# Turning layer 0's output by VectorE and DRAM instead of TensorE, in a block loop with given orders for three engines

## The chip, the cores and the metric

The kernel runs on one core of one Trainium2 chip. The metric is the device time of one execution in microseconds, as the median of several runs. TensorE (PE in the profile, its weight loads PEld), VectorE (DVE), ScalarE (ACT), GpSimd (POOL) and SyncE (SP) run their own instruction streams in order and wait for each other by semaphores. Transfers go through DMA queues; nearly all of this kernel's are issued by SyncE.

## The reference

Four layers over 128 graphs of 64 nodes with 256 features (8192 tokens), each with a residual and a layer norm. Only layers 0 and 1 are touched here:

```
# layer 0: dense graph attention
Wh = x @ W;  e = leaky(s1[:, None] + s2[None, :]);  e[adj == 0] = -inf
x = layernorm(x + softmax(e) @ Wh)
# layer 1: attention over 512 edges, 4 heads
q, v = x @ W_lin.T, x @ W_val.T
e = sum_d a * leaky(q[src] + q[dst])  + log(adj[src, dst] + 1e-8)
attn = softmax of e over the edges of one src
x = layernorm(x + segment_sum(attn * v[dst], src) @ W_out.T)
# layer 2: two batch-normed matmuls; layer 3: two graph convolutions and four small LSTMs
```

Layer 1's matmuls contract over features, so they need layer 0's output with features on the partitions, while layer 0 leaves it with tokens on the partitions. That turn is what the change is about.

## The kernel before

The 8192 tokens are cut into 16 blocks q of 512 tokens (8 graphs). Layers 0 and 1 and the start of layer 2 are one software pipeline over these blocks, from 0 to about 543 us; layer 2's matmuls and layer 3 follow and are the same in both kernels.

Layer 0 of a block is five steps. `l0_a` gives the input with features on partitions (`xT`): transfers have laid 32x32 squares of x in place in `A[:, q]`, and one VectorE instruction turns each square (L220). `l0_b` is x @ W (L230), `l0_c` the scores and their exponentials (L241 on TensorE, L244 to L248 on VectorE, L251 on ScalarE), `l0_d` transposes the exponentials on TensorE (L260) and copies them out (`eT`, L262), `l0_e` multiplies (L270), adds the residual (L273) and norms (L92 to L97). The norm's statistics are VectorE's, its power (L83) and its application (L97) GpSimd's. The result x1 stays in `A[:, q]`.

Layer 1 of a block: `l1_t` transposes x1 by eight PE transposes (L204) and two ScalarE copies (L205). `l1_qv` makes queries and values of half a block (L295, L298; copies L305 to L308). `l1_graph`, eight times a block, makes q[src] + q[dst] of one graph (`z`, L332) and its relu on ScalarE (`u`, L334). `sums` reduces four of them over the features (L323). Every second block, the softmax of the last two blocks follows: `l1_softmax` (L342 on TensorE, then a serial VectorE chain L344 to L351 with two scans, and the exponential L352), `l1_sums` (two more scans, L357 and L358) and `l1_weights` (transposes L366, reciprocal L372, product L374, four scattering transfers from GpSimd, L378, into a table in DRAM, and the load of the table back, `ld`, L384). Three to four blocks later come `v_a` (GpSimd copies the attention out of `ld` into `am`, L391; TensorE multiplies by the values, L399; ScalarE copies to `yT`, L403), `v_b` (L413, the residual add L415, the norm, the write of x2 to DRAM L418) and `v_c` (L433, copied into `A[:, q]` by L437).

The steps of a block are written out by hand: after each of the eight `l1_graph` calls b = 0 to 7 stands a short list of steps, called slot b here.

```
                [(l0_e, q + 1), (l0_a, q + 2)],
                [(sums, q if q else -1), (l1_softmax, S)],
                [(l1_sums, S), (l0_b, q + 2)],
                [(v_b, q - LAG - 1)],
                [(l1_weights, S), (l1_t, q + 1), (l0_c, q + 2)],
                [(sums, q), (l1_qv, q + 1, 0)],
                [(v_c, q - LAG - 1), (v_a, q - LAG)],
                [(l0_d, q + 2), (l1_qv, q + 1, 1)],
```

`step` holds each step behind the last TensorE instruction of the step before. The other engines' instructions are put in order by the scheduler that builds the program, by its own costs. It also picks the PSUM bank of each tile: the name "m" has three banks, "z" two, "e" one.

`A` is one tile of 16 x 1024 numbers per partition. `A[:, q]` serves in turn as the place for x's squares, for x1 and for layer 2's input. All plain transfers of the loop are issued by SyncE, in program order.

Of the kernel before, what the change touches and what calls it, by code (L numbers as in the profile page):

```python
# [17 lines left out]
P = 128  # L18
# [23 lines left out]
def kernel(ctx: ExitStack, tc: tile.TileContext, i, out):  # L42
# [69 lines left out]
    with ExitStack() as two:  # L112
# [13 lines left out]
        def load_x(q):  # L126
            xin[q] = xp.tile([P, PQ, D], F32, name="xin")
            nc.sync.dma_start(xin[q], x_view[q])
            if q:

                rows = i["x"][q * QT:(q + 1) * QT, :].rearrange("(j t) (k i f) -> i k t j f", t=32, k=KD, f=32)
                for n in range(4):
                    for k in range(KD):
                        to = A[n * 32:(n + 1) * 32, q, k * QT:(k + 1) * QT]
                        nc.sync.dma_start(to.rearrange("t (j f) -> t j f", f=32), rows[n, k])

        class su:

# [27 lines left out]
        for s in range(2):  # L166
            nc.sync.dma_start(bd[s * N:(s + 1) * N, s * N:(s + 1) * N], i["adj"])
        load_x(1)

        wq = wa.tile([P, KD, D + HEADS], F32, name="wq")  # L170
        wv = wa.tile([P, KD, D], F32, name="wv")
# [42 lines left out]

        def l0_a(q):
            L0[q] = {"x": xin.pop(q)}
            if q:

                L0[q]["xT"] = work.tile([P, KD, QT], F32, name="tT", bufs=1)
                nc.vector.transpose(L0[q]["xT"].rearrange("p k t -> p (k t)"), A[:, q, :])  # L220
            else:
                L0[q]["xT"] = transposed(L0[q]["x"], q)

        def l0_b(q):
            xT = L0[q]["xT"]
            wh = L0[q]["wh"] = own(q, [P, PQ, D + 2], "wh")
            for c in range(PQ):
                p_ = bank([D + 2])
                for k in range(KD):
                    nc.tensor.matmul(p_, xT[:, k, c * P:(c + 1) * P], w0[:, k, :],  # L230
                                     start=k == 0, stop=k == KD - 1)
                nc.scalar.activation(wh[:, c, :], p_, AF.Copy)

            sb = L0[q]["sb"] = own(q, [P, PQ, P], "sb")
            nc.scalar.activation(sb, wh[:, :, D + 1:].to_broadcast([P, PQ, P]), AF.Copy)

        def l0_c(q):
            wh, sb = L0[q]["wh"], L0[q]["sb"]
            sc = bank([PQ, P])
            for c in range(PQ):  # L240
                nc.tensor.transpose(sc[:, c, :], sb[:, c, :], ident)  # L241
            e = L0[q]["e"] = work.tile([P, PQ, P], F32, name="e0")
            for c in range(PQ):
                nc.vector.scalar_tensor_tensor(e[:, c, :], sc[:, c, :], wh[:, c, D:D + 1], mask,  # L244
                                               op0=OP.add, op1=OP.add)
            nc.vector.scalar_tensor_tensor(e, e, SLOPE, e, op0=OP.mult, op1=OP.max)
            mx = small.tile([P, PQ], F32, name="mx")
            nc.vector.tensor_reduce(mx, e, AX.X, OP.max, negate=True)  # L248
            sm = small.tile([P, PQ], F32, name="sm")
            for c in range(PQ):  # L250
                nc.scalar.activation(e[:, c, :], e[:, c, :], AF.Exp, bias=mx[:, c:c + 1],  # L251
                                     accum_out=sm[:, c:c + 1])
            ri = L0[q]["ri"] = small.tile([P, PQ], F32, name="ri")
            nc.vector.reciprocal(ri, sm)

        def l0_d(q):
            e = L0[q]["e"]
# [4 lines left out]
            nc.scalar.activation(eT, p_, AF.Copy)  # L262

        def l0_e(q):
            x, wh, eT, ri = (L0[q][n] for n in ("x", "wh", "eT", "ri"))
            for c2 in range(2):
                p_ = bank([2, D])
                for c in range(2):
                    g = 2 * c2 + c
                    nc.tensor.matmul(p_[:, c, :], eT[:, g, :], wh[:, g, :D], start=True, stop=True)  # L270
                for c in range(2):
                    g = 2 * c2 + c
                    nc.vector.scalar_tensor_tensor(x[:, g, :], p_[:, c, :], ri[:, g:g + 1], x[:, g, :],  # L273
                                                   op0=OP.mult, op1=OP.add)
            layernorm(token_major(q), x, PQ, nc.gpsimd)
            L0.pop(q)
            if q + 2 < NQ:
                load_x(q + 2)

# [1 line left out]
        L1 = {}  # L281

        def l1_t(q):
            L1[q] = {"xT": transposed(token_major(q)), "qs": [],
                     "v": vp.tile([P, PQ, D], F32, name="v", bufs=5)}

        def l1_qv(q, c2):
            xT, v = L1[q]["xT"], L1[q]["v"]
# [3 lines left out]
            for c in (2 * c2, 2 * c2 + 1):  # L292
                pq = bank([D + HEADS])
                for k in range(KD):
                    nc.tensor.matmul(pq, xT[:, k, c * P:(c + 1) * P], wq[:, k, :],  # L295
                                     start=k == 0, stop=k == KD - 1)
                for k in range(KD):
                    nc.tensor.matmul(pv[:, c % 2, :], xT[:, k, c * P:(c + 1) * P], wv[:, k, :],  # L298
                                     start=k == 0, stop=k == KD - 1)

                qs = work.tile([P, 2, D], F32R, name="qs", bufs=6)
# [37 lines left out]
        def l1_softmax(S):  # L339
# [9 lines left out]
            nc.vector.tensor_tensor_scan(up, seg[:, :E], e, NEG, OP.add, OP.max)  # L349
            nc.vector.tensor_tensor_scan(dn[:, ::-1], seg[:, 1:][:, ::-1], up[:, ::-1], NEG, OP.add, OP.max)  # L350
            nc.vector.tensor_sub(e, e, dn)  # L351
            nc.scalar.activation(e, e, AF.Exp)  # L352
            sm[S] = e, up, dn

        def l1_sums(S):
            e, up, dn = sm[S]
# [27 lines left out]
                nc.sync.dma_start(ld[S][s * N:(s + 1) * N], half)  # L384


        def v_a(q):
            S, b = divmod(q, BPS)
            v = L1[q]["v"]
            am = vp.tile([P, PQ * HEADS, N], F32, name="am")  # L390
            nc.gpsimd.tensor_copy(am.rearrange("p (e r) n -> p e r n", e=2),  # L391
                                  ld[S].rearrange("p n (e b r) -> p b e r n", e=2, b=BPS)[:, b])
            pY = [bank([KD, PQ, N]) for _ in range(2)]
            for c in range(PQ):
                for h in range(HEADS):
# [242 lines left out]
        LAG = BPS + 1  # L638


        queue = []

        def step(do, n, *more):
            if not 0 <= n < NQ:
                return
            traced = nc.cur_bb.bb.instructions
            first = len(traced)
            if queue:
                with tc.issue_after(queue[-1]):
                    do(n, *more)  # L650
            else:
                do(n, *more)
            mine = [t for t in traced[first:] if t.engine == mybir.EngineType.PE]
            queue.extend(mine[-1:])

        def sums(q):
            reduce_heads([pend.pop(0) for _ in range(min(4, len(pend)))])
# [1 line left out]
        for q in range(NQ):  # L659
            S = q // BPS - 1 if q % BPS == 0 else -1  # L660
            between = [
                [(l0_e, q + 1), (l0_a, q + 2)],
                [(sums, q if q else -1), (l1_softmax, S)],
                [(l1_sums, S), (l0_b, q + 2)],
                [(v_b, q - LAG - 1)],
                [(l1_weights, S), (l1_t, q + 1), (l0_c, q + 2)],
                [(sums, q), (l1_qv, q + 1, 0)],
                [(v_c, q - LAG - 1), (v_a, q - LAG)],
                [(l0_d, q + 2), (l1_qv, q + 1, 1)],
            ]  # L670
            for b in range(GQ):
                step(l1_graph, q, b)
# [3 lines left out]
                    setup.pop(0)()  # L676
        sums(q)
        S = NQ // BPS - 1
        for do in (l1_softmax, l1_sums, l1_weights):
            do(S)  # L680
        ph.close()

# [52 lines left out]
        q = 0  # L735
        for do, n in [(v_b, NQ - LAG - 1), (v_c, NQ - LAG - 1)] + [
                (do, n) for n in range(NQ - LAG, NQ) for do in (v_a, v_b, v_c)]:
            do(n, *[False] * (do == v_c))
            up_block(q)
            q += 1  # L740
# [397 lines left out]
```

## Time and profile before

| | before |
|---|---|
| time, median of 3 runs | 2138.03 us (2137.05 to 2138.46) |
| span of the profiled execution | 2136.4 us |
| TensorE busy | 2060.7 us |
| VectorE busy | 885.9 us |
| ScalarE busy | 932.1 us |
| GpSimd busy | 430.1 us |
| bytes moved by transfers | 113.41 MB |

A line of the profile names engine, source line, operation and what is written from what. In a timeline the first two numbers are the start and the busy time in us, and brackets tell how long the engine was idle before, and who released it. The block loop takes from about 53 to 522 us; L342 marks each softmax, and stands at 111.65, 165.75, 349.51, 410.77, 472.02 and 521.58 us among others. Two of them are a pair of blocks apart.

### The profile page before, as it was taken

Reading aid. Unit: us, or ns where it says so; the run is one execution under the profiler, and the core shown is the slowest. Engines: PE = TensorE matmul, PEld = TensorE weight load, DVE = VectorE, ACT = ScalarE, POOL = GpSimd, SP = SyncE. Lnnn points to the kernel's source line nnn. Section 1 sums busy time; section 2 is a strip of 40 time slices with the busy share of each in tenths; the row PEclk is TensorE's granted clock in tenths of the full one; section 3 lists DMA queues with packets and bytes.
Section 4 is the critical chain, followed back from the end, with each engine's and each line's share of the span. In section 5 each row is a group of like instructions: output and inputs, shape, how many; then the busy total and the mean of one; then the engine's idle time right before and its main releaser. Section 6 shows DMA issues by size and latency. Waiting matters only on the chain.

```text
span 2136.4 us, 29441 instructions
## 1 busy us (share of the span) xinstructions
PE 2060.7 (96%) x11343; PEld 1330.1 (62%) x11343; DVE 885.9 (41%) x2069; ACT 932.1 (44%) x1795; POOL 430.1 (20%) x569
## 2 busy tenths in 40 slices
PE   5999999998999989999999999999999999999998
PEld 4666767665544444585576576577467468468467
DVE  7456566654444343333234334324324324323213
ACT  2776666664339014334234334334334334333333
POOL 1134334332210010121112112113103103102012
PEclk8999999998999989999999999999999999999999
DMA  5244532322240021012112102103103102101001
GB/s 144 63 69 73 85 61 53 52 43 43 43 118 29 0 89 60 21 54 66 40 46 74 40 29 90 40 11 99 50 6 104 50 1 89 50 1 60 20 1 60
DMA packets 232636, 113.41 MB, mean 53 GB/s; under 512 B 150192, under 2 KB 215728, under 8 KB 232240
## 3 DMA queue, kind: packets, MB, share of 16 engines
q1 hardware_dynamic: 230640, 109.57, 20.2%
q8 instruction: 89, 1.46, 0.3%
q0 software_dynamic: 1024, 1.05, 0.2%
q10 hardware_dynamic: 832, 0.92, 0.1%
q14 instruction: 51, 0.42, 0.1%
HBM read 67.45 MB, written 44.04 MB: 52 GB/s over the span
## 4 chain that ended last, share of the span: by engine, by line
PE 86%; DVE 6%; ACT 4%; issue 2%; POOL 1%; DMA 1%; SPq 0%; POOLq 0%; DVEq 0%; ACTq 0%
PE l L994 36%; PE l L1000 20%; PE pz L784 5%; PE pz L719 5%; PE e L323 3%; PE g L933 2%; PE g L945 2%; PE m L295 2%; PE m L230 2%; PE z L332 2%; PE m L298 2%; PE g L878 1%; PE m L413 1%; PE m L270 1%; ACT u L334 1%
## 5 line engine op out<-in xcount | busy, mean ns | idle before, releaser
L994 PE MATMUL l<-H,wih 128*128 128x256 f32 (+2 forms) x2496 | 787.5, 470 | 1.8 <-ACT H L957 1.2
L994 PEld LDWEIGHTS l<-H,wih 128*128 128x128 f32 x2496 | 471.4, 190 | 286.2 <-issue 185.6
L1000 PE MATMUL l<-hid,whh 128*128 128x256 f32 (+2 forms) x1536 | 435.9, 437 | 0.0
L1000 PEld LDWEIGHTS l<-hid,whh 128*128 128x128 f32 x1536 | 291.8, 190 | 128.4 <-issue 61.2
L1006 ACT ACTIVATE gate_i<-l,bias 128x256 f32<-128x256 f32 (+2 forms) x176 | 100.3, 570 | 441.9 <-PE l L1000 374.2
L1010 POOL TENSOR_TENSOR cell<-gate_f,cell 128x256 f32<-128x256 f32 (+2 forms) x96 | 85.0, 885 | 726.0 <-ACT gate_f L1006 726.0
L1009 DVE TENSOR_TENSOR gate_i<-gate_i,gate_g 128x256 f32<-128x256 f32 (+2 forms) x96 | 49.6, 517 | 415.1 <-ACT gate_g L1006 415.0
L83 POOL TENSOR_TENSOR ln_rs<-ln_rs,mhalf 128x2 f32<-128x2 f32 (+2 forms) x97 | 82.0, 846 | 571.6 <-DVE ln_rs L95 570.7
L334 ACT ACTIVATE u<-z 128x1024 f32<-128x1024 f32 x128 | 130.3, 1025 | 63.3 <-PE z L332 62.3
L1006 ACT ACTIVATE gate_g<-l,bias 128x256 f32<-128x256 f32 (+2 forms) x176 | 100.3, 570 | 107.9 <-PE l L994 59.5
L1014 ACT ACTIVATE gate_g<-cell 128x256 f32<-128x256 f32 (+2 forms) x176 | 90.0, 511 | 86.9 <-DVE cell L1013 45.0
L1013 DVE TENSOR_TENSOR cell<-gate_i,gate_g 128x512 f32<-128x512 f32 (+2 forms) x80 | 48.2, 602 | 186.5 <-ACT gate_g L1006 186.4
L1006 ACT ACTIVATE gate_o<-l,bias 128x256 f32<-128x256 f32 (+2 forms) x176 | 99.3, 564 | 59.9 <-PE l L1000 54.0
L719 PE MATMUL pz<-A,w 128*128 128x512 f32 x256 | 113.1, 595 | 0.0
L332 PE MATMUL z<-gath_r,qs 128*128 128x512 f32 x256 | 100.4, 480 | 0.7 <-ACT u L334 0.4
L306 DVE TENSOR_TENSOR qs<-m,qs 64x256 fp32r<-64x256 f32 x128 | 54.0, 422 | 107.0 <-ACT qs L305 104.8
L719 PEld LDWEIGHTS pz<-A,w 128*128 128x128 f32 x256 | 47.9, 190 | 55.3 <-issue 53.3
L295 PE MATMUL m<-wq,tT 128*128 128x260 f32 x256 | 71.8, 403 | 7.8 <-ACT yT L403 5.4
L1006 ACT ACTIVATE gate_f<-l,bias 128x256 f32<-128x256 f32 (+2 forms) x96 | 51.1, 532 | 59.6 <-PE l L1000 59.1
L1023 DVE TENSOR_TENSOR hid<-gate_o,gate_g 128x256 f32<-128x256 f32 (+2 forms) x96 | 47.4, 493 | 61.2 <-ACT gate_o L1006 35.1
L721 DVE BATCH_NORM_STATS2 st<-pz 128x6 f32<-128x512 f32 x64 | 44.4, 697 | 59.5 <-PE pz L719 59.4
L1023 DVE TENSOR_TENSOR H<-gate_o,gate_g 128x512 f32<-128x512 f32 (+1 forms) x64 | 41.3, 645 | 66.6 <-PE l L994 46.1
(242 smaller groups left out, 2525.2 us busy)
## 6 DMA issues: line engine op xcount, KB each, us to landing
way<-st SPq DMA_DIRECT2D x59, 256.0 KB
st<-way SPq DMA_DIRECT2D x236, 64.0 KB
xin<-in_x SPq DMA_DIRECT2D x16, 512.0 KB
ld<-table SPq DMA_DIRECT2D x16, 512.0 KB
x_dram<-y SPq DMA_DIRECT2D x16, 512.0 KB
x2r<-x_dram SPq DMA_DIRECT2D x32, 256.0 KB
x_dram<-A SPq DMA_DIRECT2D x64, 128.0 KB
x3r<-x_dram SPq DMA_DIRECT2D x64, 128.0 KB
```

The lines of the kernel that those rows point to most:

```text
L83: nc.gpsimd.tensor_tensor(dst, dst, mhalf[:, :n], OP.pow)
L295: nc.tensor.matmul(pq, xT[:, k, c * P:(c + 1) * P], wq[:, k, :], start=k == 0, stop=k == KD - 1)
L332: nc.tensor.matmul(z[:, k, :], L1[q]["qs"][c][:, s, k * P:(k + 1) * P], gath_r, start=True, stop=True)
L334: nc.scalar.activation(u, z, AF.Relu)
L719: nc.tensor.matmul(p_, w1[:, k, m * P:(m + 1) * P], A[:, q, k * QT:(k + 1) * QT], start=k == 0, stop=k == KD - 1)
L784: nc.tensor.matmul(p_, w2[:, k, m * P:(m + 1) * P], hidden(q, k), start=k == 0, stop=k == M1 - 1)
L994: nc.tensor.matmul(gates[n], wih[p][:, k, mw * P:(mw + 1) * P], Hw[:, k, :, s, :], start=k == 0, stop=not s and k == KD - 1)
L1000: nc.tensor.matmul(gates[n], whh[p][:, k, m * P:(m + 1) * P], hid[:, k], start=False, stop=k == KD - 1)
L1006: nc.scalar.activation(act[n], gates[n], AF.Tanh if n == "g" else AF.Sigmoid, bias=bias[:, p - 1, m:m + 1])
L1010: nc.gpsimd.tensor_tensor(cell[:, j], act["f"], cell[:, j], OP.mult)
L1014: nc.scalar.activation(act["g"], cell[:, j], AF.Tanh)
L1023: nc.vector.tensor_mul(Hw[:, jj, :, s, :] if over else new[:, jj], o, t)
```

## The change

Layer 0's output is no longer transposed by TensorE for blocks 2 to 15. Instead, x1 is written to DRAM as it is, read back as 32x32 squares by eight transfers (`load_squares`), and turned by one VectorE instruction, as layer 0's input is. The aim is to take the eight transposes and the two ScalarE copies away. Blocks 0 and 1 keep the TensorE way, and block 1's input, turned by VectorE before, goes that way too.

The squares need a place. Layer 0's input is now turned from `A[:, q]` into `A[:, q + 1]`, and x1's squares land in `A[:, q + 1]` once that is free; so x's own squares are loaded later than before, one block at a time, after `l0_b` of the block before.

The slots are rearranged, and `step` now holds TensorE, VectorE and GpSimd, each behind its last instruction of the steps before. The softmax's exponential is a step of its own (`l1_exp`), and so is GpSimd's copy of the attention (`v_am`), which now stands ahead of `v_b` and its norm. Layer 0's reciprocal moves from `l0_c` to `l0_e`.

```diff
+        TURN = 2
+
+        def load_squares(to, rows):
...
+        def load_xT(q):
+
+            load_squares(A[:, q, :], i["x"][q * QT:(q + 1) * QT, :])
...
         load_x(1)
+        load_xT(2)
...
-            if q:
-
-                L0[q]["xT"] = work.tile([P, KD, QT], F32, name="tT", bufs=1)
-                nc.vector.transpose(L0[q]["xT"].rearrange("p k t -> p (k t)"), A[:, q, :])
-            else:
+            if q < TURN:
                 L0[q]["xT"] = transposed(L0[q]["x"], q)
+                return
+
+            t = A[:, q + 1, :] if q + 1 < NQ else work.tile([P, KD * QT], F32, name="tT", bufs=1)
+            nc.vector.transpose(t, A[:, q, :])
+            L0[q]["xT"] = t.rearrange("p (k t) -> p k t", k=KD)
...
             nc.scalar.activation(sb, wh[:, :, D + 1:].to_broadcast([P, PQ, P]), AF.Copy)
+            if TURN <= q + 1 < NQ:
+                load_xT(q + 1)
...
             layernorm(token_major(q), x, PQ, nc.gpsimd)
             L0.pop(q)
+            if q >= TURN:
+
+                x1 = dram.tile([QT, D], F32, name="x1_dram", bufs=2)
+                nc.sync.dma_start(x1.rearrange("(c p) d -> p c d", p=P), token_major(q))
+                sq[q] = A[:, q + 1, :] if q + 2 < NQ else xp.tile([P, PQ, D], F32, name="xin").rearrange(
+                    "p c d -> p (c d)")
+                load_squares(sq[q], x1)
...
         def l1_t(q):
...
+            xT = work.tile([P, KD, QT], F32, name="tT", bufs=1)
+            nc.vector.transpose(xT.rearrange("p k t -> p (k t)"), sq.pop(q))
...
-            nc.scalar.activation(e, e, AF.Exp)
             sm[S] = e, up, dn
+
+        def l1_exp(S):
+
+            with tc.issue_after([t for t in nc.cur_bb.bb.instructions if t.engine == mybir.EngineType.Activation][-1]):
+                nc.scalar.activation(sm[S][0], sm[S][0], AF.Exp)
...
-        def v_a(q):
+        def v_am(q):
             S, b = divmod(q, BPS)
...
-        queue = []
+
+        latest = {}
...
-            if queue:
-                with tc.issue_after(queue[-1]):
-                    do(n, *more)
-            else:
+            with ExitStack() as order:
+                for t in latest.values():
+                    order.enter_context(tc.issue_after(t))
                 do(n, *more)
-            mine = [t for t in traced[first:] if t.engine == mybir.EngineType.PE]
-            queue.extend(mine[-1:])
+            for t in traced[first:]:
+                if t.engine in (mybir.EngineType.PE, mybir.EngineType.DVE, mybir.EngineType.Pool):
+                    latest[t.engine] = t
...
-                [(l0_e, q + 1), (l0_a, q + 2)],
-                [(sums, q if q else -1), (l1_softmax, S)],
-                [(l1_sums, S), (l0_b, q + 2)],
-                [(v_b, q - LAG - 1)],
-                [(l1_weights, S), (l1_t, q + 1), (l0_c, q + 2)],
-                [(sums, q), (l1_qv, q + 1, 0)],
-                [(v_c, q - LAG - 1), (v_a, q - LAG)],
-                [(l0_d, q + 2), (l1_qv, q + 1, 1)],
+                [(l0_e, -1 if q else 1), (l0_a, -1 if q else 2), (l1_qv, q if q else -1, 1)],
+                [(sums, q if q else -1), (l1_softmax, S), (l0_b, q + 2), (l1_exp, S), (v_am, q - LAG)],
+                [(l1_sums, S), (v_b, q - LAG - 1)],
+                [(l0_c, q + 2), (l1_t, -1 if q else 1)],
+                [(l1_t, q + 1 if q else -1), (l1_weights, S)],
+                [(sums, q), (v_a, q - LAG)],
+                [(l0_d, q + 2), (l1_qv, q + 1, 0)],
+                [(v_c, q - LAG - 1), (l0_a, q + 3 if q + 4 < NQ else -1), (l0_e, q + 2),
+                 (l0_a, q + 3 if q + 4 == NQ else -1)],
```

## The prediction

> **What bounds the kernel now.** I read the page first (engine shares), then the busy times by stretch, then the waits of TensorE in the block loop, then the timeline of one pair of blocks, and last the issues of SyncE.
>
> ```profile
> PE 2060.7 (96%) x11343; PEld 1330.1 (62%) x11343; DVE 885.9 (41%) x2069; ACT 932.1 (44%) x1795; POOL 430.1 (20%) x569
> ```
>
> TensorE is the bound at 96%. So a change pays where TensorE waits or works less, and nowhere else. The change touches only the set-up and the block loop (to 543 us), so the next view is by stretch: two pairs of blocks, then the last two blocks and the drain after the loop (length; PE, PEld, DVE, ACT and POOL busy; granted clock, DMA share, GB/s).
>
> ```profile
> 227.00:288.00 61.00, 58.01 (x542) 42.96 (x538) 37.22 (x95) 40.90 (x91) 23.43 (x26) 1.00 0.48 80
> 288.00:349.00 61.00, 58.01 (x542) 42.96 (x538) 37.23 (x96) 40.90 (x91) 23.42 (x26) 1.00 0.30 55
> ...
> 472.00:522.00 50.00, 43.41 (x435) 27.25 (x432) 19.58 (x48) 24.99 (x41) 19.86 (x21) 0.86 0.30 46
> 522.00:543.00 21.00, 17.09 (x113) 9.13 (x112) 15.20 (x28) 4.07 (x6) 6.66 (x9) 1.00 0.02 5
> ```
>
> A pair is 61 us with 58 us of matmuls: only 3 us are idle, at full clock. The last two blocks are the loose ones, 43 busy of 50 at a clock of 0.86. TensorE's waits between 227 and 472 us name the idle time (four pairs; us in total, times, longest):
>
> ```profile
> PE m L295 <- ACT yT L403: 4.3, 8, 0.6
> PE m L204 <- ACT tT L205: 2.8, 4, 0.7
> PE m L204 <- issue: 2.7, 4, 0.7
> PE m L241 <- DVE ln_mv L93: 1.8, 4, 0.5
> ```
>
> Of the 11.6 us, 5.5 belong to the transposes L204 that the change removes. The timeline of the pair at 349 us shows where they stand, and the VectorE chain that starts at L342:
>
> ```profile
> 349.51 1.13 PE L342 MATMUL e<-gath,spad 128*128 128x512 f32 x2
> ...
> 350.68 0.69 DVE L344 TENSOR_TENSOR e<-e,lb 128x512 f32<-128x512 f32 x1
> ...
> 357.04 1.22 DVE L358 TENSOR_TENSOR_SCAN dn<-seg,up 128x512 f32<-128x512 f32 x1
> ...
> 360.52 0.79 PE L204 MATMUL m<-ident,A 128*128 128x128 f32 x4 [0.67 <-issue]
> ...
> 362.00 0.65 PE L204 MATMUL m<-ident,A 128*128 128x128 f32 x4 [0.69 <-ACT tT L205]
> ...
> 376.78 3.33 SPq L384 DMA_DIRECT2D ld<-table  x2
> ...
> 387.15 1.98 POOL L391 COPY am<-ld 128x1024 f32<-128x1024 f32 x1 [0.49 <-DMA ld<-table]
> ```
>
> From L342 to the end of L358 VectorE is busy for 7.6 us on one serial chain; L204's two halves each wait in an even block; and the attention table lands 10.4 us after its issue, with GpSimd waiting for it. SyncE's issues price the new transfers: eight "squares" in 5.2 us, and four that start at 245.91.
>
> ```profile
> 42.98 5.23 SPq L135 DMA_DIRECT2D A<-in_x  x8
> ...
> 245.91 2.54 SPq L135 DMA_DIRECT2D A<-in_x  x4
> ```
>
> The chain has the last of those landing at 249.65, 1.2 us after its issue ended.
>
> **What the Trainium skill says.** "VectorE: DVE Perf Modes", The three transpose paths: VectorE transposes 32x32 blocks only, into SBUF. The trace agrees: it turns 128x1024 in 1.245 us (L220), after squares were laid out by transfers. "DMA: Bandwidth & Descriptors", Queues, rings and completion order: on each DMA engine the descriptors of one issuing engine are consumed in ring order. No view of before separates the landings of two transfers that stand behind each other, so no run here shows it yet. "TensorE: Matmul & The Clock Gate", Part 4: PE transposes don't count as busy for the clock gate. The trace agrees in kind: around 118 to 124 us, with transposes and 2.07 us idle, L323 took 2.41 us instead of 1.92.
>
> **The change, part by part.** I call q = 4, 6, ... 12 even blocks (they carry a softmax), the others odd; E0 and O0 are the starts of their first z. What each engine meets in which order is read from the built program, the durations from the timeline. From the starts of TensorE's rows in the pair: z 0.65, reduce of four 1.86, half of the queries and values 3.4, L230 3.3, L413 3.3, L241 and L260 0.6 each, L366 1.1, L399 1.17, L433 0.98, L270 1.54, L342 0.56.
>
> Removed, for q >= 2: eight PE transposes of layer 0's output (0.88 us back to back at 390.7) and two ACT copies of 0.6. The pair without them sums to 28.9 (even) + 27.2 (odd) = 56.1 us; that agrees with 58.1 less 2.3 of L204. So up to 5.2 us per pair could go. Added: one 1.25 us transpose on VectorE per block, a 512 KB write and 8 squares on SyncE. Moved: layer 0's scores to slot 3, its turn of the attention (l0_d) to slot 6, v_a to slot 5, and VectorE and GpSimd keep program order.
>
> Even block, on VectorE. The reduce and L342 are reached at 0.65 + 3.4 + 0.65 + 1.86 = E0+6.55 (call it T0). L344 starts 1.17 later (349.51 to 350.68), L358 ends 7.58 after that: T0+8.75. In the given order the residual add and its statistics follow (3.46 from 389.13 to 392.59): T0+12.15, then layer 0's scores (2.57, from 392.59 to 395.16): maxima at T0+14.7. ScalarE's four exponentials take 1.66: T0+16.4. Before, these scores were wanted last of all (l0_d in slot 7); now they are wanted in slot 6, ahead of the queries. And there is a bank: the two softmax transposes hold two of the three "m" banks until VectorE has done the new transpose, the reciprocal (1.73) and the product (0.9), T0+18.6. The built program puts both halves of v_a, then l0_d, then the first query matmul into the one bank left, and ScalarE's copies yT stand behind the exponentials. So: copy 0.55, second half 0.6, copy 0.55, z beside it, transposes 0.65, u 1.0, eT 0.65, with hand-overs: queries start at T0+20.25. TensorE alone would be there at T0+15.7 (0.56, 3.3, 0.65, 3.3, 0.65, 0.6, 0.65, 1.1, 0.65, 1.86, 1.17, 0.65, 0.57). Stall 4.55; even block 28.9 + 4.55 = 33.4 us. The 2 us that even blocks idle before (at L204 and L241) are gone, so the net loss is smaller than the stall.
>
> Odd block. L95 of layer 0's norm ends at O0+3.9 (as 87.96 after a start at 84.05), GpSimd's power and norm take 3.2: the write of x1 is issued at O0+7.3. But the table load ld stands before it on SyncE. In the even block the scatters start at T0+18.3, the fourth 9.5 later (123.64 to 133.11), ld 2.15 after that: T0+30 = O0+3.1, O0 being T0+26.9. It moved data for 9.0 us (376.8 to 385.8), until O0+12. In ring order x1's write then needs 2 us of data (368.8 to 371 for the same 512 KB) and 1.3 to be seen (385.8 to 387.15): O0+15.4. Squares 5.2 + 1.2, transpose 1.25: xT at O0+23.1. TensorE could use it at O0+20.6. Stall 2.5; odd block 29.7 us. If the transfers share evenly instead, x1 is there by O0+12 and only ScalarE's eT makes TensorE wait, 0.6: 27.8 us. I take ring order, and keep both ends.
>
> GpSimd's copy am waits for ld, ready at O0+13.5, done O0+15.5; behind it stands the residual's norm, whose input comes at O0+15.8; v_a wants am at O0+18.2. No cost. In the last block am is late for both before and after. In even blocks x1 lands at E0+18, VectorE comes to it at E0+21.2: hidden.
>
> Pair: 33.4 + 29.7 = 63.1 against 61.26 (349.51 to 410.77): +1.9, five times: +9.5. Block 1 has no residual step to cover x1's way (landed at its start + 17.5, turned at 18.8, wanted at 17.5): 1.3 of wait less 0.9 of transposes, +0.4. In block 3, with no residual step either, am comes 3.9 after v_a wants it and xT, behind ld, 5.2 after the queries do: blocks 2 and 3 take 58.8 against 54.1 (L342 at 111.65 and 165.75), +4.7; shared, +1. Blocks 14 and 15, with no layer 0: before 49.5 (L342 at 472.0 and 521.6), now 46 to 48 (transposes and their waits out, am still 4 late): -3.5 to -1.5; I take -3. Set-up: x1's turn goes from VectorE to TensorE (1 us among other waits of both): 0. Sum +11.6; I round to +10, as the first pairs may hide a little: 2148.
>
> **The rivals.**
> A. The banks and the order cost nothing, TensorE runs through: pairs at 57.1 (56.1 and 1 of small waits), -4.1 x 5 - 3.5: 2114. For it: VectorE and ScalarE are free over 20 us of each pair. Against it: the chain from L342 is serial, and its durations are in the trace.
> B. Even blocks as worked out, transfers shared: pairs 61.2, so 0 + 0.4 + 1 - 3: 2136 to 2138, no change. For it: the DMA share stood at 1.2 to 1.6 during ld, several transfers overlapped within an engine.
> C. As forecast, and the clock falls in the even block's gaps, where transposes stand between two idle stretches: 2 us a pair (L323 and its neighbours around 122 us lost 1.6, around 484 us 2.3), +10: 2158. Against it: no gap there reaches 3 us.
>
> **How the numbers follow.** Forecast 0.45, A 0.15, B 0.25, C 0.15. The range leaves out A and some of C: 2131 to 2160. Faster by over 0.2% (under 2133.8): A and a fifth of B, 0.20. Within 0.2%: most of B and the forecast's low end, 0.22. Slower: 0.58.
>
> **What would show it.** Right: in even blocks TensorE waits at the second half of v_a, l0_d and the first query matmul for yT and eT, 4 to 5 us; in odd blocks the transpose of x1 waits for transfers and xT comes at O0+23; pair period 63 us; 472 to 522 shorter. Wrong: a pair under 60 us, a maxima row earlier than T0+14, or x1's squares landing by O0+19 in odd blocks.

## The result, and the profile after

The changed kernel takes 2162.74 us (median of four, 2156.2 to 2165.65), the kernel before 2138.24 beside it: a ratio of 1.0111, 95% interval 1.0085 to 1.0136. The forecast of 2148.0 had the direction right and the size too small by 14.7 us; the time lies 2.7 us above its range.

The engine shares, from the page of the changed kernel:

```profile
PE 2068.3 (96%) x11239; PEld 1333.0 (62%) x11239; DVE 900.0 (42%) x2082; ACT 917.3 (42%) x1769; POOL 414.7 (19%) x569
```

TensorE has 104 instructions less than before (11343) and is busy 7.6 us longer (2060.7). Matmuls that became longer with the same shapes point at the clock, so the stretches come next: blocks 2 and 3, then five pairs, cut at the softmax matmul L368 (length; PE, PEld, DVE, ACT, POOL busy; granted clock, DMA share, GB/s).

```profile
114.00:176.20 62.20, 51.66 (x303) 35.40 (x299) 32.91 (x74) 36.94 (x85) 12.46 (x16) 0.92 0.52 87
176.20:241.40 65.20, 61.18 (x527) 44.41 (x523) 39.74 (x97) 39.06 (x88) 21.86 (x28) 0.95 0.54 100
241.40:305.80 64.40, 60.67 (x526) 44.17 (x522) 39.52 (x97) 38.88 (x88) 21.51 (x27) 0.95 0.55 101
305.80:369.80 64.00, 60.69 (x526) 44.19 (x522) 39.45 (x97) 39.03 (x88) 21.57 (x27) 0.95 0.52 102
369.80:431.90 62.10, 58.21 (x527) 42.44 (x523) 39.62 (x97) 38.99 (x88) 21.60 (x27) 1.00 0.53 105
431.90:496.70 64.80, 61.05 (x526) 44.38 (x522) 38.61 (x96) 39.46 (x89) 22.02 (x28) 0.95 0.46 84
```

The granted clock, third from the end, is what to read: 1.00 is TensorE's full speed. One pair ran at full clock and took 62.06 us (369.83 to 431.89); four ran at 0.95 and took 64.0 to 65.2. Before, the pairs took 61.25 us, at a clock of 1.00 up to 472 us.

Where the 22.4 us between the two profiled spans come from, cut at the softmax matmuls:

| stretch | before | after | difference | forecast |
|---|---|---|---|---|
| start to the first softmax (block 2) | 111.65 | 114.03 | +2.4 | +0.4 |
| blocks 2 and 3, to the second | 54.10 | 62.15 | +8.05 | +4.7 |
| five pairs | 306.27 | 320.56 | +14.3 | +9.5 |
| blocks 14 and 15 | 49.56 | 46.19 | -3.4 | -3 |
| the rest | 1614.82 | 1615.87 | +1.05 | 0 |

TensorE's waits over the five pairs (us in total, times, longest):

```profile
PE m L431 <- ACT yT L435: 9.3, 5, 1.9
PE m L321 <- ACT eT L273: 3.8, 5, 0.9
PE m L396 <- DVE y L447: 2.2, 5, 0.6
```

The first two are the second half of `v_a` and the first query matmul of the even blocks, as forecast; no odd block waits for x1. The timeline of the pair at full clock shows both halves of the forecast:

```profile
369.83 1.12 PE L368 MATMUL e<-gath,spad 128*128 128x512 f32 x2
...
377.34 1.23 DVE L388 TENSOR_TENSOR_SCAN dn<-seg,up 128x512 f32<-128x512 f32 x1
...
383.60 0.69 DVE L261 TENSOR_REDUCE mx<-e 128x4 f32<-128x512 f32 x1
...
384.20 1.24 DVE L310 STREAM_TRANSPOSE tT<-A 128x1024 f32<-128x1024 f32 x1
...
385.36 1.72 DVE L402 RECIPROCAL rd<-m 128x256 f32<-128x256 f32 x1
...
386.50 1.15 PE L431 MATMUL m<-am,v 64*64 64x64 f32 x32 [1.86 <-ACT yT L435]
...
389.92 1.14 PE L321 MATMUL m<-wq,tT 128*128 128x260 f32 x4 [0.91 <-ACT eT L273]
...
403.99 2.61 SPq L293 DMA_DIRECT2D x_dram<-A  x1
...
410.39 4.04 SPq L138 DMA_DIRECT2D A<-x_dram  x8
...
416.39 1.25 DVE L310 STREAM_TRANSPOSE tT<-A 128x1024 f32<-128x1024 f32 x1 [0.28 <-DMA A<-in_x]
```

With T0 = 369.83, the scans end at T0+8.74, the maxima at T0+14.5, and the first query matmul starts at T0+20.1: the even block's chain runs as forecast, within 0.25 us. In the odd block (O0 = 397.43), x1 is turned at O0+20.2, 3 us earlier than forecast and in time.

The same place one pair earlier, at the low clock:

```profile
322.49 1.15 PE L431 MATMUL m<-am,v 64*64 64x64 f32 x32 [1.85 <-ACT yT L435]
323.57 0.80 PE L358 MATMUL z<-gath_r,qs 128*128 128x512 f32 x2
324.33 1.12 PE L271 MATMUL m<-ident,e 128*128 128x128 f32 x4
326.14 2.10 PE L321 MATMUL m<-wq,tT 128*128 128x260 f32 x4 [0.69 <-ACT eT L273]
328.03 2.77 PE L324 MATMUL m<-wv,tT 128*128 128x256 f32 x6
```

Four query matmuls take 2.10 us instead of 1.14, the six of L324 2.77 instead of 1.46. The waits are no longer than in the pair at full clock; only the matmuls after them are slower. Block 3 has longer waits, for the table load and for x1, and a longer slow stretch after them:

```profile
153.65 1.99 PE L431 MATMUL m<-am,v 64*64 64x64 f32 x64 [3.21 <-POOL am L420]
...
161.14 2.07 PE L321 MATMUL m<-wq,tT 128*128 128x260 f32 x4 [3.83 <-DVE tT L310]
163.00 1.91 PE L324 MATMUL m<-wv,tT 128*128 128x256 f32 x4
```

### The profile page after: what moved, and what is told of

It is laid out like the page before. It is cut to its first block, busy times and chain, and to the rows that moved or that the text cites. A ratio compares the mean times of both kernels' runs of the same rounds, so it can differ in the third digit from the quotient of the medians.

```text
span 2158.8 us, 29496 instructions
## 1 busy us (share of the span) xinstructions
PE 2068.3 (96%) x11239; PEld 1333.0 (62%) x11239; DVE 900.0 (42%) x2082; ACT 917.3 (42%) x1769; POOL 414.7 (19%) x569
## 3 DMA queue, kind: packets, MB, share of 16 engines
q0 software_dynamic: 1024, 1.05, 0.2%
## 4 chain that ended last, share of the span: by engine, by line
PE 84%; DVE 6%; ACT 3%; DMA 3%; issue 2%; POOL 1%; SPq 1%; POOLq 0%; DVEq 0%; ACTq 0%
PE l L1030 35%; PE l L1036 19%; PE pz L820 5%; PE pz L753 5%; PE m L321 3%; PE g L969 2%; PE g L981 2%; PE m L241 2%; PE m L324 2%; PE g L914 1%; PE m L283 1%; PE z L358 1%; PE e L349 1%; DVE ln_st L92 1%; ACT e L264 1%
## 5 line engine op out<-in xcount | busy, mean ns | idle before, releaser
L321 PE MATMUL m<-wq,tT 128*128 128x260 f32 x256 | 77.0, 428 | 13.3 <-ACT eT L273 4.8
L324 PE MATMUL m<-wv,tT 128*128 128x256 f32 x256 | 73.6, 415 | 0.0
L321 PEld LDWEIGHTS m<-wq,tT 128*128 128x128 f32 x256 | 52.1, 212 | 27.6 <-ACT eT L273 8.2
```

Of the source, the lines that this page charges most:

```text
L321: nc.tensor.matmul(pq, xT[k][c], wq[:, k, :], start=k == 0, stop=k == KD - 1)
L324: nc.tensor.matmul(pv[:, c % 2, :], xT[k][c], wv[:, k, :], start=k == 0, stop=k == KD - 1)
```

## The experiments

Theory: the waits of the even block and of block 3 are about as forecast, and the clock that falls after them makes the rest of the cost. Rivals: the transfers make the pairs long; the given orders do; the low clock only goes along with the waits. Line numbers move by a few from kernel to kernel; "even" and "odd" lengths are from one block's first z to the next.

**e1: the orders without the turn.** `l1_t` uses TensorE in all blocks, the write and the squares are out.

```diff
-            if q < TURN:
+            if True:
                 xT = transposed(token_major(q))
...
-            if q >= TURN:
...
-                load_squares(sq[q], x1)
```

> The changed kernel with its slots and its three orders, but x1 turned by TensorE in all blocks: no x1 write, no squares, no VectorE turn of x1. Theory (the single free bank of the even block costs the time, whoever turns x1): the first query matmul of even blocks still starts about 20 us after the softmax matmul, pairs take 62 to 64 us (0.9 us of transposes more in each odd block, hidden in the even block's stall), block 3 loses its 3.8 us wait for x1's squares; sum 2153 to 2166. Rival (the way through DRAM costs the time): pairs go back to 61.3 us or less, the total to 2140 to 2146.

2130.35 us, ratio 0.9959 (0.9945 to 0.9973): below both kernels and both expectations. Even blocks take 31.7 us, odd ones 28.2, blocks 2 and 3 51.7. e1 keeps all the rest of the change, the later loading of x's squares too. So slots and orders with that rest win 8 us, and the turn through DRAM loses 32 on top of them. The theory as put here is wrong in one point: the even block's stall is not there "whoever turns x1". VectorE's row list shows why: with no turn of x1 behind the maxima, the reciprocal follows at once, `v_a` waits only 0.49 us for its bank, and the queries don't wait for `eT`.

```profile
360.54 0.69 DVE L261 TENSOR_REDUCE mx<-e 128x4 f32<-128x512 f32 x1
361.15 1.75 DVE L395 RECIPROCAL rd<-m 128x256 f32<-128x256 f32 x1
...
362.95 1.15 PE L424 MATMUL m<-am,v 64*64 64x64 f32 x50 [0.49 <-DVE rd L395]
...
365.05 1.04 PE L314 MATMUL m<-wq,tT 128*128 128x260 f32 x4
```

The softmax matmul is at 346.78 here, so the queries start at T0+18.3 instead of T0+20.1.

**e2: the waits filled.** The changed kernel, with matmuls of no use in TensorE's waits.

```diff
-                [(sums, q), (v_a, q - LAG)],
-                [(l0_d, q + 2), (l1_qv, q + 1, 0)],
+                [(sums, q), (warm, lone, 8), (v_a, q - LAG, (0,)), (warm, soft, 4), (v_a, q - LAG, (1,))],
+                [(l0_d, q + 2), (warm, soft, 2), (warm, lone, 9), (l1_qv, q + 1, 0)],
```

`soft` is set in even blocks from the fourth on, `lone` in block 3; the last number counts the matmuls, and `v_a` is cut into its halves.

> The changed kernel with matmuls of no use put where TensorE waits: four between the halves of v_a and two before the first query matmul of each even block, eight and nine before the same two places in block 3; they write a z bank that nobody reads. Theory (the granted clock falls to half after these waits and costs 2 to 2.5 us in four of five pairs and 4 us in block 3): the clock reads 1.00 in all pairs, pairs take 62.0 to 62.4 us, blocks 2 and 3 about 59 us; total 2147 to 2153. Rival (the low clock reading goes along with the waits and costs nothing by itself): pairs stay at 64 to 65 us, total 2158 to 2168.

2153.7 us, ratio 1.0068 (1.0051 to 1.0084), 9 us below the changed kernel, 0.7 above the range expected and well under the rival's; the pairs take 62.6, 61.5, 61.4, 62.1 and 63.9 us at a clock of 1.00. L440 are the useless matmuls:

```profile
313.78 1.15 PE L431 MATMUL m<-am,v 64*64 64x64 f32 x32
314.86 1.20 PE L440 MATMUL z<-gath_r,qs 128*128 128x512 f32 x4
316.79 1.15 PE L431 MATMUL m<-am,v 64*64 64x64 f32 x32 [0.73 <-ACT yT L435]
...
319.05 0.71 PE L440 MATMUL z<-gath_r,qs 128*128 128x512 f32 x2
320.20 1.14 PE L321 MATMUL m<-wq,tT 128*128 128x260 f32 x4 [0.44 <-ACT eT L273]
321.18 1.46 PE L324 MATMUL m<-wv,tT 128*128 128x256 f32 x6
```

The softmax matmul is at 300.12. The second half of `v_a` starts at T0+16.67, as in the changed kernel (386.50 - 369.83), the first query matmul at T0+20.08, as there. The same holds in block 3: counted from the softmax before it, `v_a` starts at 39.9 us (39.6 in the changed kernel) and the first query matmul at 47.2 (47.1). These two places, where TensorE waited, start no earlier for the added work; only the clock after them differs. So the low clock is a cost of its own. By the two profiles, the five pairs and blocks 2 and 3 are 11.4 us shorter together; the set-up, where nothing was filled, is 2.2 longer. The cut of `v_a` into halves was not run alone.

**e3: banks freed first.** Weights ahead of x1's turn and of the scores, `l0_d` in slot 7.

```diff
-                [(l0_c, q + 2), (l1_t, -1 if q else 1)],
-                [(l1_t, q + 1 if q else -1), (l1_weights, S)],
+                [(l1_weights, S), (l1_t, -1 if q else 1)],
+                [(l1_t, q + 1 if q else -1), (l0_c, q + 2)],
...
-                [(l0_d, q + 2), (l1_qv, q + 1, 0)],
+                [(l1_qv, q + 1, 0)],
```

> The changed kernel with other slots: the softmax weights stand before the turn of x1 and layer 0's scores, so that VectorE frees their two banks first; the turn of layer 0's attention stands in slot 7, behind the first half of the queries. Theory (one free bank and a VectorE chain in front of it make the even block's stall): v_a's second half waits for no yT copy, the first query matmul of an even block starts 16 to 17 us after the softmax matmul instead of 20, the clock stays at 1.00 there, pairs take 57.5 to 59 us; total 2126 to 2138. Rival (VectorE's chain is too long in any order, and layer 0's attention is then late for its product in slot 7): the wait moves to that product, pairs 61 to 63 us, total 2150 to 2160.

2170.1 us, ratio 1.0142 (1.0125 to 1.0159): slower, neither expectation. The queries of even blocks do start at T0+16.4, and most even blocks take 31.7 us; but the odd blocks grew from 27.9 to between 31.4 and 34.7. TensorE now waits there for x1 and for `eT`:

```profile
PE m L321 <- DVE tT L310: 13.4, 5, 4.5
PE m L283 <- ACT eT L273: 10.1, 10, 2.5
```

The total says little of the pairs, though: the first softmax comes at 124.08 instead of 114.03, which is 10 of the 11 us between the two profiled spans, and the five pairs together are only 2 us longer. Still, the odd block's wait for x1, which the forecast had, does exist: the even block's stall had hidden it by giving the transfers time.

**e4: x1's write on another queue.**

```diff
-                nc.sync.dma_start(x1.rearrange("(c p) d -> p c d", p=P), token_major(q))
+                nc.scalar.dma_start(x1.rearrange("(c p) d -> p c d", p=P), token_major(q))
```

> The changed kernel with x1's write to DRAM issued by ScalarE instead of SyncE, so that it doesn't stand behind the table load on one ring. Theory (ring order holds it back): in odd blocks the squares are issued at about 10 us after the block's first z instead of 13, and block 3's turn of x1 comes 3 to 4 us earlier; pairs keep their length within 0.5 us, since x1 was in time there; total 2154 to 2160. Rival (the two transfers share the engines, the order makes no difference): squares issued at 12 to 13 us as before, total 2160 to 2165.

2168.09 us, ratio 1.0134 (1.0114 to 1.0153): no gain, and above both ranges. In the pair shown, the squares, which wait for the write, are issued 4.4 us after its issue began instead of 6.4 (403.99 to 410.39 in the changed kernel). The third line is the copy that waits for the table load:

```profile
405.45 0.37 ACTq L293 DMA_DIRECT2D x_dram<-A  x1
409.86 4.03 SPq L138 DMA_DIRECT2D A<-x_dram  x8
411.50 2.01 POOL L420 COPY am<-ld 128x1024 f32<-128x1024 f32 x1 [6.08 <-DMA ld<-table]
```

The same copy in the changed kernel:

```profile
409.42 1.97 POOL L420 COPY am<-ld 128x1024 f32<-128x1024 f32 x1 [5.46 <-DMA ld<-table]
```

So with its own queue the write lands before the table load, 1.6 us here, where on SyncE's it landed 1.0 after it. The order turns in the other odd blocks too, wherever the copy shows when the load was there: write first in four of four here, last in five of five in the changed kernel. Ring order (one queue's transfers in the order of issue) did hold x1 back, as the forecast had it. But little was won: over the six odd blocks the squares follow the start of the write's issue by 5.0 us on average instead of 5.5. The Trainium skill, "DMA: Bandwidth & Descriptors", Issuing engines are not separate DMA queues, says that several issuing engines save only the time of issuing. In the pair shown that agrees (0.37 us instead of 2.61); the turned order of landing comes on top of it. In block 3 the theory came out: x1's turn starts 20.7 us after the block's first z instead of 25.2, TensorE's 3.83 us of wait for it are gone, and the block takes 29.7 us instead of 35.1, though it now waits 3.0 us for ScalarE at L241. What this wins is lost elsewhere: the first softmax comes 3.4 us later, and the last two blocks take 4.3 us more. ScalarE, which now stands at the issue until GpSimd's norm is done, also makes TensorE wait: 6.4 us in the pairs in eight waits at L241 for `spad`, which the changed kernel didn't have.

**e5: weights ahead of x1's turn,** the rest as changed.

```diff
-                [(l1_t, q + 1 if q else -1), (l1_weights, S)],
+                [(l1_weights, S), (l1_t, q + 1 if q else -1)],
```

> The changed kernel with one pair of steps swapped: the softmax weights stand ahead of the turn of x1 in slot 4, so that VectorE's reciprocal and product, which free two banks, no longer wait behind the 1.25 us turn. Theory (in the even block TensorE waits for these banks, and behind that for x1's way through DRAM in the odd block): even blocks fall from 34 to 37 us to about 32, v_a's second half goes into a freed bank; odd blocks grow from 27.9 to 29 to 32 us, because the next x1 now comes too late for TensorE; pairs 61 to 64 us, total 2148 to 2162. Rival (the bank wait is the whole cost of a pair): odd blocks stay at 27.9 us, pairs about 60 us, total 2138 to 2144.

2155.62 us, ratio 1.0083 (1.0068 to 1.0099), 7 us less. Even blocks take 33.2 us, at a clock of 0.97 in the pairs; odd ones stay at 28 to 29. The total is as expected. The growth of the odd blocks stayed under 1 us, though TensorE does wait for x1 now, 2.9 us in three places; the last two blocks grew from 46.2 to 49.9.

**e6: VectorE's turn alone,** added to e1.

```diff
                 xT = transposed(token_major(q))
+                if TURN <= q < NQ - 2:
+                    nc.vector.transpose(A[:, q + 1, :], A[:, q, :])
```

> The kernel with x1 turned by TensorE and the three orders (2130 us), and in addition the VectorE turn alone: a 128x1024 transpose that nobody reads, at the same place in VectorE's order, without x1's write and squares. Theory (VectorE's turn ahead of the reciprocal holds the two banks): even blocks grow from 31.7 to 33 to 36 us, odd ones stay at 28; total 2138 to 2152. Rival (the transfers cost the time, not VectorE's turn): even blocks within 0.5 us, total 2129 to 2134.

2139.66 us, ratio 1.0004 (0.9995 to 1.0012): 9.3 us above e1. Even blocks take 32.7 us in three pairs and 34.3 and 35.2 in the two where the clock read 0.97; odd ones stay at 28. In e1 the first of the two slow ones had taken 32.7 and the other 31.7. So 1.25 us of VectorE in the wrong place made an even block 1.0 us longer, and the clock took 1.6 more in each of two pairs. `v_a` waits 1.15 us for its bank in all five.

**e7: squares from the input;** layer 1 then gets layer 0's input.

```diff
-                load_squares(sq[q], x1)
+                load_squares(sq[q], i["x"][q * QT:(q + 1) * QT, :])
```

> The changed kernel with x1's squares read from the input x, which is in DRAM from the start, instead of from the x1 just written; x1's write stays. So layer 1 gets layer 0's input in place of its output, and the squares no longer wait for the write to land. Theory (in pairs the squares are in time, only block 3 waits for them): pairs stay at 62 to 65 us, block 3 loses up to 3.8 us of wait and 1 to 2 us of low clock; total 2155 to 2160. Rival (the round trip through DRAM makes the pairs long): pairs 60 to 61.5 us, total under 2148.

2146.18 us, ratio 1.0039 (1.0023 to 1.0055), lower than the theory had it. Block 3 fell from 35.1 to 31.2 us, as expected; but even blocks fell to 33.7 at a clock of 0.97 (the first to 35.5). The wait of `v_a` stayed (9.3 us in five), while the first query matmul no longer waited for `eT`: so it no longer goes into that bank. The run changed two things and doesn't tell them apart in the pairs.

**e8: a better version.** e1 with block 2's input turned ahead of block 1's norm.

```diff
-                [(l0_e, -1 if q else 1), (l0_a, -1 if q else 2), (l1_qv, q if q else -1, 1)],
+                [(l0_a, -1 if q else 2), (l0_e, -1 if q else 1), (l1_qv, q if q else -1, 1)],
```

> The kernel with x1 turned by TensorE and the three orders (2130 us), with two steps of the first block swapped: block 2's input is turned ahead of block 1's residual and norm on VectorE. Theory (the order on VectorE makes TensorE wait 3.9 us for that turn near 57 us, and run at a low clock after it): the first softmax matmul comes at 110 to 112.5 us instead of 115; total 2125 to 2128. Rival (other set-up work ends there at the same time): the first softmax matmul at 114 to 115.5, total 2129 to 2132.

2122.65 us, ratio 0.9926 (0.9912 to 0.9939): faster than both kernels, and by more than expected. The first softmax matmul comes at 106.93 instead of 115.08 in e1. In the changed kernel the same order shows as

```profile
59.59 6.23 PE L241 MATMUL m<-w,A 128*128 128x258 f32 x16 [3.90 <-DVE A L232]
```

a wait of 3.9 us and then sixteen matmuls at the low clock (3.65 us at full clock). **e12** makes this swap alone in the changed kernel:

> The changed kernel with only the set-up swap: block 2's input is turned ahead of block 1's residual and norm on VectorE. Theory (the given VectorE order costs 8 us in the set-up, whoever turns x1): the first softmax matmul at 106 to 108 us instead of 114, total 2153 to 2157. Rival (with the turn through DRAM other work fills that time): first softmax matmul at 112 to 114, total 2160 to 2164.

2150.47 us, ratio 1.0073 (1.0058 to 1.0087), first softmax matmul at 107.05, as expected: 7 us earlier than in the changed kernel. The total is 12 us lower, below the range expected. The rest lies in blocks 2 and 3 (2.5 less) and in the pairs (61.4 to 65.7 us), where the clock differs from pair to pair.

**e9: the turn without the orders.** The slots of before (except as below), and only TensorE's order.

```diff
-                if t.engine in (mybir.EngineType.PE, mybir.EngineType.DVE, mybir.EngineType.Pool):
+                if t.engine in (mybir.EngineType.PE,):
...
+                [(l0_a, q + 2), (l0_e, q + 1)],
+                [(sums, q if q else -1), (l1_softmax, S), (l1_exp, S)],
```

> The turn through DRAM and VectorE without the given orders: the slots of the kernel before (with layer 0's turn of its input ahead of its product), and only TensorE's order held. Theory (x1 is written in slot 0 and wanted in slot 5, some 15 to 19 us later, which its write, squares and turn of about 11 us after the norm at 7 us don't fit): the first query matmul waits for VectorE's turn by 2 to 4 us in odd blocks and the clock falls after it; pairs 62 to 66 us, total 2145 to 2170. Rival (the orders and slots of the change are what costs, the turn alone is hidden): pairs 59 to 61 us, total 2125 to 2140.

2202.81 us, ratio 1.0312 (1.0298 to 1.0327), worse than either expectation. From the waits of TensorE between 170 and 480 us:

```profile
PE m L321 <- DVE tT L310: 43.2, 8, 6.3
```

Both kinds of block wait for x1. So the change's slots and orders, taken together, are what makes the turn bearable: they save 40 us with it and 8 without it.

**e10: queries ahead of `l0_d`** in slot 6, and **e11: e10, e5 and e12 together.**

```diff
-                [(l0_d, q + 2), (l1_qv, q + 1, 0)],
+                [(l1_qv, q + 1, 0), (l0_d, q + 2)],
```

> The changed kernel with two steps of slot 6 swapped: the first half of the queries stands ahead of the turn of layer 0's attention, so the first query matmul no longer goes into the bank of that turn. The wait of v_a's second half stays. Theory (the one bank through which everything goes costs the even block, and the transfers don't): first query matmul 18 to 19 us after the softmax matmul instead of 20, even blocks 32 to 34 us, odd ones 28; total 2145 to 2156. Rival (x1's transfers set the pair): odd blocks grow by what even ones lose, total 2158 to 2166.

> The turn through DRAM with what the runs so far showed: softmax weights ahead of x1's turn, queries ahead of layer 0's attention, block 2's input turned first in the set-up. Theory: even blocks about 32 us, odd ones 28 to 29, 8 us less in the set-up; total 2134 to 2145, still above the TensorE turn (2122.7), because block 3 still waits for the table load and x1. Rival (with the banks free the turn through DRAM wins its 1.8 us of transposes a pair): total under 2122.

e10: 2160.97 us (2155.57 to 2161.77), ratio 1.0119 (1.0104 to 1.0134), not told from the changed kernel and in the rival's range. Even blocks take 32.9 to 36.0 us, and TensorE now waits 4.0 us in four places for x1's turn. e11: 2144.39 us, ratio 1.0041 (1.0027 to 1.0056): the best of the turns through DRAM, and still above the kernel before.

**e13: the transfers alone.** e1 with x1's write and squares, read by nobody. **e14: e11 with its waits filled.**

```diff
+                [(sums, q), (warm, lone, 8), (v_a, q - LAG, (0,)), (warm, soft, 3), (v_a, q - LAG, (1,))],
+                [(warm, soft, 1), (warm, lone, 8), (l1_qv, q + 1, 0), (l0_d, q + 2)],
```

> The kernel with x1 turned by TensorE and the three orders (2130 us), and in addition x1's write to DRAM and its squares, which nobody reads; no VectorE turn of x1. Theory (transfers cost only where somebody waits for them: the table load in block 3, and GpSimd's copy behind it, come 1 to 3 us later): pairs stay at 59.7 to 60.5 us, total 2131 to 2137. Rival (the transfers slow the pairs by sharing the DMA engines with the table load): pairs 61 to 63 us, total 2140 to 2150.

> The turn through DRAM with softmax weights ahead of x1's turn, queries ahead of layer 0's attention and block 2's input first (2144 us), and with matmuls of no use in the waits of even blocks (three and one) and of block 3 (eight and eight). Theory (what is left of the cost is mostly the low clock after the waits): clock 1.00 in the pairs, pairs 60.5 to 61.5 us, total 2131 to 2138, still above the TensorE turn's 2122.7. Rival (waits for x1 and the table are left, and the useless matmuls delay as much as the clock gives): total 2142 to 2150.

e13: 2134.64 us, ratio 0.9981 (0.9974 to 0.9988), 4.3 us above e1; its even blocks take 31.7 to 32.0 us but for the first (36.4). Most of the cost lies in that one block, where TensorE waits and the matmuls after the wait are slow:

```profile
162.89 1.13 PE L324 MATMUL m<-wv,tT 128*128 128x256 f32 x4 [2.71 <-DVE xin L286]
```

In e1 this wait was 0.40. VectorE's add L286 is late because the turn before it waited for squares of x, and seven of these are issued behind x1's. So the transfers by themselves cost only where they push back another transfer that is waited for. e14: 2151.27 us, ratio 1.0059 (1.0041 to 1.0077), a miss, above both ranges. Its even blocks take 32.2 us, and three odd blocks now 30.3 to 35.9, because they wait for x1:

```profile
330.01 3.88 SPq L293 DMA_DIRECT2D x_dram<-A  x1
...
337.71 5.71 SPq L138 DMA_DIRECT2D A<-x_dram  x8
...
345.49 1.25 DVE L310 STREAM_TRANSPOSE tT<-A 128x1024 f32<-128x1024 f32 x1 [5.35 <-DMA A<-in_x]
```

GpSimd's norm ended at 328.49; the way through DRAM took 18.2 us to the end of the turn. In the changed kernel's pair above it took 13.7 (403.96 to 417.64). Why x1 comes later here stays open.

| | TensorE turns x1 | turn through DRAM |
|---|---|---|
| slots and order of before | 2138 | 2203 (e9) |
| the change's slots and orders | 2130 (e1) | 2163 |
| and block 2's input first | 2123 (e8) | 2150 (e12) |

The first row is not quite one kernel: e9 also loads x's squares as the change does, and turns its input first.

## Why the prediction was off

**Right: the even block's chain.** Scans T0+8.75 forecast, 8.74 measured; maxima 14.7 and 14.5; first query matmul 20.25 and 20.1. The even block at full clock takes 34.1 us (33.4 forecast); 0.6 of this lie at a break in L465 (0.31 us on "issue"), which e2's even blocks of 33.5 don't have. One sum is off: from the exponentials at T0+16.4, the terms listed lead to T0+20.4 before any hand-over, so the match within 0.2 us is in part luck. e5 and e6 show that VectorE's turn of x1 ahead of the reciprocal is part of the cause: without its 1.25 us `v_a` waits 0.5 us for its bank, with it 1.15.

**Wrong step: the clock, kept out of the sum.** Rival C had "2 us a pair", set aside because "no gap there reaches 3 us". The gaps are as short as that says (1.86 and 0.7 to 0.9 us, with transposes in between), and the clock fell after them in four pairs of five. The view of before gave no ground for 3 us: there the clock fell to 0.77 (121 to 124 us) and 0.66 (to 127) around waits of 2.07 and 0.69 us, the place that the prediction itself cites:

```profile
120.59 0.63 PE L366 MATMUL m<-ident,dn 128*128 128x128 f32 x4 [2.07 <-DVE dn L358]
...
122.34 0.92 PE L204 MATMUL m<-ident,A 128*128 128x128 f32 x4 [0.69 <-ACT tT L205]
...
124.97 2.41 PE L323 MATMUL e<-u,apad 128*32 128x512 f32 x16
```

Against the pair at full clock, the other pairs are longer by 3.1, 2.4, 2.0 and 2.8 us: 10.3 of the pairs' 14.3. In block 3, the two stretches of rows from 153.65 to 167.44 take 4.0 us longer than the same rows at full clock, and L241 in the set-up 2.6. That is about 17 us which the sum of 11.6 didn't have. e2, which filled the waits of the even blocks and of block 3, is 9 us faster. C in full, 2158, was the nearest of the four cases, in part by luck: it too had the odd block's stall, which didn't come, and it left out the clock in block 3 and in the set-up.

**Wrong step: "Odd block. ... Stall 2.5".** It was 0: 27.9 us against 29.7, which is what rival B had (27.8). The table load was issued 0.8 us sooner after T0 than forecast, O0 came 0.7 later, x1 was there about 1 us after the load instead of 2, and its squares 6.0 us later instead of 6.4. Together that is the 2.9 us by which x1 was turned early. The ring order behind the step was right (e4): x1 landed behind the load. The parts of the last term were not: the squares took 4.0 us to issue and 2.0 to land, against 5.2 and 1.2. The wait itself is real, and appears when the even block gets shorter (e3, e14).

**Blocks 2 and 3.** The waits in block 3 are near the forecast (3.2 for `am`, 3.9 forecast; 3.8 for x1, 5.2 forecast). The 8.05 us are the 4.7 forecast and 3.4 more; the clock after the waits takes 4.0.

**Wrong step: "Set-up: ... 0".** The given VectorE order makes TensorE wait for block 2's input. The net difference to before is only +2.4, since the changed kernel had been ahead by then (its z at 54.86, before 59.10), but the swap alone brings the first softmax 7 to 8 us forward (e8, e12).

**Right: blocks 14 and 15** (-3.4, -3 forecast), and **GpSimd's order,** which makes no wait in the pairs. Of the 32 us that the turn costs on top of the orders, VectorE's turn alone makes 9.3 and the transfers alone 4.3. The other 19 appear only where both are there and the queries need what they bring. Block 3's wait for x1, the banks that the scheduler then picks, and the clock are the parts that the runs show; how they share the 19 wasn't separated. The banks can't be chosen by hand in this kernel, and e7 and e10 moved them together with other things.

## What to carry to other kernels

A matmul less pays only if what replaces it isn't on a longer way: eight transposes of 0.9 us in all gave way to a round trip of 14 to 18 us, which needs that much slack in every block. When a sum of waits is made for TensorE, add what the clock does after each wait; filling a wait with useless matmuls is a cheap test for it, though not always a cure (e2 gained 9 us, e14 lost 7 against e11). And take a change apart into its orders and its new way before judging it: here one half was worth keeping and the other not.

## What the runs showed of the hardware

The granted clock can fall after waits of 1.9 us and less: after 1.86 and 0.7 to 0.9 us in the changed kernel, where it read 0.50 from 326.2 to 330.5 us, and after 1.15 us in e6. Whether it does differs from pair to pair with the same waits (four of five, and two of five). The Trainium skill, "TensorE: Matmul & The Clock Gate", Part 1, describes a free-running window of some 3.4 us, so that its phase against the work varies; that fits the change from pair to pair. It speaks of a whole idle window, and no gap in the pairs is that long. But around the wait stand only 64x64 matmuls. Counted with them, from the first matmul of `v_a` to the next z, the stretch is 2.2 us in e1 and e13, where the clock held in all ten pairs; at full clock it is 3.4 in e6 (fell in two of five), 3.6 in e5 (all five) and 4.1 in the changed kernel (four of five). That would fit the window if the 64x64 matmuls counted as idle, which no run here tests.

e11, with such waits, spread widely, 2139.6 to 2157.0 us in twelve runs, and e8 from 2121.7 to 2123.5 in five. But e9, which waits longest of all, spread from 2201.9 to 2203.8 in four: waits alone don't make the spread.

The issue of a transfer on SyncE can itself be long: x1's write took 0.38 us to issue in even blocks (370.30), 0.39 to 3.94 in odd ones behind the table load, and 2.61 and 3.94 where it followed the load's issue at once (403.99, 145.07). All that SyncE issues next waits as long.

x1's write landed after the table load that was issued before it on SyncE's queue (five odd blocks of five), and ahead of it when ScalarE issued it (four of four, e4).
